# Spike counts and membrane reset of a spiking recurrence: bfloat16 count on VectorE, spike taken from v - 1 written by ScalarE

## The chip, the core and the metric

The kernel runs on one core of a Trainium2 chip. The metric is the device time in microseconds, median of several executions. The engines that appear below are PE (TensorE, matrix products and transposes), VectorE (DVE), ScalarE (ACT), GpSimd (POOL, here the issuer of the gathers) and SyncE (SP, issuer of the stores). They run their own instruction streams and wait for one another through semaphores. SBUF is the on-chip memory, PSUM the eight banks that PE writes its results to.

## The reference

Of the reference only one sequence model matters: 1024 sequences of 50 item numbers, a table of 100001 embeddings of 128 numbers, scores for all items.

```python
emb = emb_table.at[0].set(0.0)
e = emb[seq]                                   # (1024, 50, 128)
prefix = jnp.cumsum(e, axis=1)
denom = jnp.minimum(t_idx[None, :], lengths[:, None])
uF = prefix / denom[:, :, None]
mean = uF.mean(axis=0)
var = uF.var(axis=0)
y = (uF - mean) * lax.rsqrt(var + BN_EPS) * gamma + beta
def step(v, x):
    v = v + (x - v) / TAU                      # TAU = 2
    spike = atan_spike(v - V_TH)               # 1 where v >= 1
    v = v - lax.stop_gradient(spike) * V_TH
    return (v, spike)
_, spikes = lax.scan(step, v0, x_seq)          # 50 steps
uF_out = spikes.mean(axis=0)                   # (1024, 128)
scores = uF_out @ emb.T                        # (1024, 100001)
```

So for each of 50 steps the running mean of the gathered embeddings is normalised over the batch, fed into a leaky integrator with a threshold, and the spikes are counted. The counts, divided by 50, are multiplied with the whole table.

## The kernel before

The kernel has two stages. In the first, the recurrence, everything lies transposed: 128 embedding dimensions on the partitions, 1024 sequences along the row, in two halves of 512 that fit a PSUM bank each. In the second the counts are the stationary operand and the table, split into a high and a low part, is multiplied with them block by block, scaled by 1/50 on VectorE and ScalarE in turn (L469, L471), and stored by SP (L161).

The order of the instructions on each engine is that of the program; nothing reorders them. For the recurrence it is written by hand. Step t of the loop (L288) does this:

- POOL issues the eight gathers of step t + 2 (L194), 128 table rows each, into one of three buffers e. It may begin when the transposes of step t - 1 have read that buffer.
- PE transposes the eight blocks of e(t) and adds them to the running sum in PSUM, `pre[0]` and `pre[1]` (L301). A correction by PE (`correct`, L257) takes out row 0 of the table in advance; its factor l is made by ScalarE (`only`, L252).
- VectorE multiplies each half with the reciprocal length (L310, giving uF) and takes batch statistics of it (L311), then the mean and the variance mv (L321).
- ScalarE takes the square root (L325) and subtracts the mean from uF (L326). Meanwhile VectorE computes s, the spikes of the previous step, as bfloat16 zeros and ones from v in PSUM (L331), and PE adds them up by a product with the identity matrix (`counted`, L268) into two PSUM banks `sums` over all steps.
- VectorE finishes the scale a of the normalisation (L334 to L340).
- ScalarE writes x, the scaled uF, into the PSUM tile v of this step (`x`, L344; v lies in two tiles in turn, v0 and v1). Meanwhile VectorE computes negv = s - v of the previous step (L353).
- VectorE finishes the step, v = x - negv/2 (`step`, L347).

The sign of negv makes the reset and the leak one operation. In the last step, t = 49, s and negv of step 48 are computed at the top of the loop's body (L295, L296), and the sums of steps 0 to 48 are copied from PSUM by ScalarE into a tile `count` (L319). The spikes of step 49 are added to it in three groups of columns (`spiked`, L279), which gives the operands of the products. Before these, PE runs sixteen transposes of the identity matrix (`warm`, L378) while it waits.

In steps 42 and 44 the first two blocks of the table are also transposed and split (`prepare`, L122, L144, L145), with tile v1 as their place in PSUM.

The two lines on which the counting rests before:

```python
nc.vector.tensor_single_scalar(s, v, V_TH, ALU.is_ge)
nc.vector.tensor_tensor(negv, s, v, ALU.subtract)
```

Of the kernel before, what the change touches and what calls it, by code (L numbers as in the profile page):

```python
# [12 lines left out]
F32 = mybir.dt.float32  # L13
BF16 = mybir.dt.bfloat16
# [3 lines left out]
AF = mybir.ActivationFunctionType  # L18
ALU = mybir.AluOpType

P = 128
BN_EPS = 1e-5
V_TH = 1.0
HALF = 1024
KQ = HALF // P
BANK = 512
# [9 lines left out]
def rec_kernel(  # L36
# [9 lines left out]
    nc = tc.nc  # L46
    B, T = seq.shape
# [20 lines left out]
    ident = const.tile([P, P], F32, tag="ident", name="ident")  # L68
# [80 lines left out]
    def product(po, q, n, k0, kw):  # L149
        kw += kw % 2  # L150
        for j, part in enumerate(split[q]):
            nc.tensor.matmul(  # L152
                po[:, :kw],
                lhsT=counts[n],
                rhs=part[:, k0 : k0 + kw],
                start=j == 0,
                stop=j == 1,
            )
# [4 lines left out]

    with ExitStack() as ph:
        once = ph.enter_context(tc.tile_pool(name="once", bufs=1))
        lp = ph.enter_context(tc.tile_pool(name="lif", bufs=2))
        sp = ph.enter_context(tc.tile_pool(name="stats", bufs=3))
        up = ph.enter_context(tc.tile_pool(name="uF", bufs=2))
        gp = ph.enter_context(tc.tile_pool(name="gather", bufs=3))
        accp = ph.enter_context(tc.tile_pool(name="acc", bufs=1, space=bass.MemoryType.PSUM))  # L170
# [20 lines left out]
        def gather(t):  # L191
            es[t] = gp.tile([P, B], F32, tag="e", name=f"e_{t}")
            for n in range(NB):
                nc.gpsimd.indirect_dma_start(  # L194
                    out=es[t][:, n * P : (n + 1) * P],
                    out_offset=None,
                    in_=table,
                    in_offset=bass.IndirectOffsetOnAxis(ap=idx[:, n, t : t + 1].bitcast(U32), axis=0),
                )
# [12 lines left out]
        zT = once.tile([P, B], F32R, tag="zT", name="zT")  # L212
# [23 lines left out]
        nc.vector.tensor_scalar_mul(hgb[:, 1:2], gb[:, 1:2], 0.5)  # L236
        eps = once.tile([P, 1], F32, tag="eps", name="eps")
        nc.vector.memset(eps, BN_EPS)
        ident_h = once.tile([P, P], BF16, tag="ident_h", name="ident_h")
        nc.vector.tensor_copy(ident_h, ident)  # L240

        negv = once.tile([P, B], F32, tag="negv", name="negv")
        nc.vector.memset(negv, 0.0)


        pre = [accp.tile([P, BANK], F32, tag=f"pre{h}", name=f"pre{h}") for h in range(B // BANK)]
        sums = [accp.tile([P, BANK], F32, tag=f"sums{h}", name=f"sums{h}") for h in range(B // BANK)]

        def only(t):

# [12 lines left out]
                    skip_group_check=True,  # L263
                )

        def counted(t, s):
            for h in range(B // BANK):
                nc.tensor.matmul(  # L268
                    sums[h],
                    lhsT=ident_h,  # L270
                    rhs=s[:, h * BANK : (h + 1) * BANK],
                    start=t == 0,
                    stop=t == T - 2,
                    skip_group_check=True,
                )


        def spiked(out, cs, v):
            nc.vector.scalar_tensor_tensor(out, v, V_TH, count[:, cs], ALU.is_ge, ALU.add)  # L279

        whole = slice(0, B)
        halves = [slice(h * BANK, (h + 1) * BANK) for h in range(B // BANK)]
        v = None
# [4 lines left out]
        for t in range(T):  # L288
            last = t == T - 1
            if t + 2 < T:  # L290
                gather(t + 2)
            e = es.pop(t)
            if last:
                s = lp.tile([P, B], BF16, tag="s", name=f"s_{t - 1}")
                nc.vector.tensor_single_scalar(s, v, V_TH, ALU.is_ge)  # L295
                nc.vector.tensor_tensor(negv, s, v, ALU.subtract)  # L296
            uF = up.tile([P, B], F32, tag="uF", name=f"uF_{t}")
            bs = sp.tile([P, B // BANK, 6], F32, tag="bs", name=f"bs_{t}")
            for h, cs in enumerate(halves):
                for k in range(0, BANK, P):  # L300
                    nc.tensor.matmul(  # L301
                        pre[h][:, k : k + P],
                        lhsT=e[:, h * BANK + k : h * BANK + k + P],
                        rhs=ident,
                        start=False,
                        stop=last,
                        is_transpose=True,
                        skip_group_check=True,
                    )
                nc.vector.scalar_tensor_tensor(uF[:, cs], rlen[:, cs], 1.0 / (t + 1), pre[h], ALU.max, ALU.mult)  # L310
                nc.vector.bn_stats(bs[:, h, :], uF[:, cs])  # L311
            if not last:
                correct(t + 1, l)
            else:

                counted(t - 1, s)
                count = once.tile([P, B], F32, tag="zT", name="count")
                for h, cs in enumerate(halves):
                    nc.scalar.copy(count[:, cs], sums[h])  # L319
            mv = sp.tile([P, 2], F32, tag="mv", name=f"mv_{t}")  # L320
            nc.vector.bn_aggr(mv, bs.rearrange("p h s -> p (h s)"))  # L321


            r = sp.tile([P, 1], F32, tag="r", name=f"r_{t}")
            nc.scalar.activation(r, mv[:, 1:2], AF.Sqrt, bias=eps)  # L325
            nc.scalar.activation(uF, uF, AF.Identity, bias=mv[:, 0:1], scale=-1.0)  # L326


            if t and not last:
                s = lp.tile([P, B], BF16, tag="s", name=f"s_{t - 1}")  # L330
                nc.vector.tensor_single_scalar(s, v, V_TH, ALU.is_ge)  # L331
                counted(t - 1, s)

            nc.vector.reciprocal(r, r)  # L334
            q = sp.tile([P, 1], F32, tag="q", name=f"q_{t}")
            nc.vector.tensor_mul(q, r, r)  # L336
            nc.vector.scalar_tensor_tensor(q, mv[:, 1:2], BN_EPS, q, ALU.add, ALU.mult)  # L337
            nc.vector.tensor_scalar(q, q, -0.5, 1.5, ALU.mult, ALU.add)
            a = sp.tile([P, 1], F32, tag="a", name=f"a_{t}")
            nc.vector.tensor_scalar(a, q, r, hgb[:, 0:1], ALU.mult, ALU.mult)  # L340


            def x(vt, cs):
                nc.scalar.activation(vt, uF[:, cs], AF.Identity, bias=hgb[:, 1:2], scale=a)  # L344

            def step(vt, cs):
                nc.vector.scalar_tensor_tensor(vt, negv[:, cs], -0.5, vt, ALU.mult, ALU.add)  # L347

            if not last:
                vt = vp.tile([P, B], F32, tag=f"v{t % 2}", name=f"v_{t}")  # L350
                x(vt, whole)
                if t:
                    nc.vector.tensor_tensor(negv, s, v, ALU.subtract)  # L353
                step(vt, whole)
                v = vt
                if t + 2 < T:
                    l = only(t + 2)

                if t in (T - 8, T - 6):
                    q = (t - T + 8) // 2  # L360
                    pair(q)
                    prepare(q, vp.tile([P, HALF], F32, tag="v1", name=f"pt_{q}"))
                    if q == TWICE - 1:
                        for k in range(TWICE):
                            rows[GROUP + k] = first[:, k, :]
                        nc.sync.dma_start(
                            out=first[:, :TWICE, :],
                            in_=table[GROUP * HALF : (GROUP + TWICE) * HALF, :].rearrange(
                                "(q p k) d -> p q (k d)", p=P, k=KQ
                            ),  # L370
                        )
# [15 lines left out]
        cs, vt, first = groups[0]  # L387
# [5 lines left out]
            spiked(c, cs, vt)  # L393


        po1 = vp.tile([P, HALF], F32, tag="v0", name="po_0_1")
        for q, (pool, tag, po) in enumerate(((gp, "e", sums), (up, "uF", [po1[:, cs] for cs in halves]))):
            o = pool.tile([P, HALF], F32, tag=tag, name=f"o_0_{q}")
            for h, cs in enumerate(halves):
                product(po[h], q, 0, h * BANK, BANK)  # L400
            for h, cs in enumerate(halves):
                if q and h:
                    nc.vector.tensor_scalar_mul(o[:, cs], po[h], 1.0 / T)
                else:
                    nc.scalar.mul(o[:, cs], po[h], 1.0 / T)
                store(0, q * HALF + h * BANK, o[:, cs])


# [16 lines left out]
    for c, W in enumerate(WIDTHS):  # L425
# [30 lines left out]
        for n in range(NB):  # L456
            if c == 0 and n == 0:
                continue
            pool, tag, most = turns[blocks % len(turns)]
            blocks += 1  # L460
            o = pool.tile([P, most * HALF], F32, tag=tag, name=f"o_{c}_{n}")
            for q in range(q0, q1):
                h0 = (q - q0) * HALF
                hw = size(q)
                po = psum.tile([P, HALF], F32, tag="ps", name=f"po_{n}_{q}")
# [45 lines left out]
```

## Time and profile before

| | us |
|---|---|
| median of three runs | 1652.33 (1652.13 to 1652.79) |
| the profiled execution | 1650.34 |
| its span, first to last instruction | 1648.6 |
| VectorE busy | 940.2 (57%) |
| PE busy | 1101.3 (67%) |
| ScalarE busy | 631.1 (38%) |
| POOL busy | 378.4 (23%) |
| gathers, L194, 400 of them | 377.7, mean 0.944 |
| spikes s, L331, 48 of them in the loop | 56.2, mean 1.170 |
| negv, L353, 48 | 58.1, mean 1.211 |
| step, L347, 47 | 57.8, mean 1.229 |
| counting on PE, L268, 128x512 each | mean 0.606 |

How to read the views: the page cuts the span into 40 slices, each digit the busy share of an engine in a slice in tenths. A timeline line gives start, length, engine, line of the program, operation, tiles written and read, and in brackets how long the engine had been idle before and what released it. "issue" means that the profile shows nothing that it waited for, "remote" that the releasing instruction wasn't found. In the chain of waits the same case is called "another core or an unknown queue"; here there is one core only. A table of stages gives, after the length of the stretch, busy time and number of instructions of PE, its weight loads, VectorE, ScalarE and POOL, then the granted clock of PE, the busy share of the DMA engines and GB/s. The records of matrix products are partly modelled: their starts and ends can lie before the real ones.

### The profile page before, as it was taken

The page shows a single profiled execution, that of the slowest core. Times are in us where ns is not written, and L with a number is a line of the kernel's source. Part 1 is how long each engine was busy: PE and PEld are TensorE (multiplying, and loading weights), DVE is VectorE, ACT ScalarE, POOL GpSimd, SP SyncE. Part 2 cuts the span into 40 slices and gives each one's busy share as a digit, 9 for nine tenths or more (in the row PEclk, how much of TensorE's full clock was granted, in tenths as well). Part 3 has the DMA queues.
Part 4 walks back from the last instruction along what each step waited for, and adds up shares of the span by engine and source line. Part 5 has one row for each costly group of instructions (what it writes and reads, how often), then busy time and mean ns, then how long its engine had stood idle before and what let it go on. Part 6 is the DMA issues. An engine that isn't in the chain of part 4 may idle for free.

```text
span 1648.6 us, 12553 instructions
## 1 busy us (share of the span) xinstructions
PE 1101.3 (67%) x4538; PEld 825.5 (50%) x4548; DVE 940.2 (57%) x1161; ACT 631.1 (38%) x700; POOL 378.4 (23%) x406
## 2 busy tenths in 40 slices
PE   3333443333333488888987887888787887888884
PEld 2112222122222366666876666666666666666763
DVE  4556666566656766556755555555555555555552
ACT  2222222222222355445544444444444444444442
POOL 7666666666666500000000000000000000000000
PEclk6555555555555589999999999989989999999998
DMA  9511111111111269999999999999999999999998
GB/s 341 214 48 43 48 47 48 48 43 48 48 47 45 64 275 417 403 423 416 399 429 427 431 432 424 422 422 418 421 427 423 430 417 410 427 427 423 396 429 343
DMA packets 53691, 488.14 MB, mean 296 GB/s; under 512 B 11995, under 2 KB 12796, under 8 KB 32380
## 3 DMA queue, kind: packets, MB, share of 16 engines
q1 hardware_dynamic: 32256, 429.81, 62.1%
q0 software_dynamic: 12800, 26.24, 5.9%
q10 hardware_dynamic: 8572, 31.28, 4.7%
q8 instruction: 36, 0.59, 0.1%
q14 instruction: 27, 0.22, 0.0%
HBM read 77.69 MB, written 409.60 MB: 296 GB/s over the span
## 4 chain that ended last, share of the span: by engine, by line
DMA 47%; DVE 22%; another core or an unknown queue 10%; PE 10%; ACT 6%; issue 4%; POOL 0%; ACTq 0%; DVEq 0%; SPq 0%
DMA scores<-o 46%; PE po L152 9%; ACT o L471 5%; DVE bs L311 4%; DVE uF L310 4%; DVE v L347 4%; DVE s L331 3%; DVE negv L353 3%; DVE o L469 1%; DVE a L340 1%; DVE mv L321 1%; ACT v L344 1%; DVE q L337 0%; DVE q L336 0%
## 5 line engine op out<-in xcount | busy, mean ns | idle before, releaser
L469 DVE TENSOR_SCALAR o<-po 128x1024 f32<-128x1024 f32 x391 | 464.1, 1221 | 351.3 <-DMA scores<-o 311.3
L471 ACT ACTIVATE o<-po 128x1024 f32<-128x1024 f32 (+1 forms) x391 | 389.1, 1018 | 542.9 <-DMA scores<-o 325.5
L194 POOL DMA_INDIRECT e<-in_L_rec_emb_table,idx x400 | 377.7, 944 | 188.2 <-issue 114.9
L152 PE MATMUL po<-pairs,countB 128*128 128x512 f32 x1136 | 306.3, 416 | 63.2 <-ACT o L471 46.5
L152 PEld LDWEIGHTS po<-pairs,countB 128*128 128x128 f32 x1136 | 219.3, 198 | 126.3 <-ACT o L471 61.2
L152 PE MATMUL po<-pairs,countC 128*128 128x512 f32 x852 | 229.7, 415 | 55.0 <-ACT o L471 54.9
L257 PE MATMUL pre<-zT,l 128*128 128x512 f32 x100 | 74.7, 749 | 275.6 <-DVE uF L310 188.6
L152 PEld LDWEIGHTS po<-pairs,countC 128*128 128x128 f32 x852 | 162.3, 197 | 99.5 <-ACT o L471 66.6
L257 PEld LDWEIGHTS pre<-zT,l 128*128 128x128 f32 x100 | 27.7, 279 | 316.9 <-issue 210.7
L310 DVE SCALAR_TENSOR_TENSOR uF<-rlen,pre 128x512 f32<-128x512 f32 x100 | 68.0, 680 | 185.3 <-remote 144.1
L325 ACT ACTIVATE r<-mv,eps 128x1 f32<-128x1 f32 x50 | 14.7, 295 | 383.5 <-DVE mv L321 266.3
L145 DVE TENSOR_TENSOR pairs<-pt,pairs 128x1024 fp32r<-128x1024 f32 x71 | 86.3, 1222 | 89.6 <-ACT pairs L144 89.5
L122 PE MATMUL pt<-ident,rows 128*128 128x128 f32 x782 | 109.4, 286 | 5.0 <-issue 3.2
L122 PEld LDWEIGHTS pt<-ident,rows 128*128 128x128 f32 x782 | 99.2, 150 | 23.3 <-issue 8.4
L301 PE MATMUL pre<-ident,e 128*128 128x128 f32 x400 | 98.4, 419 | 10.8 <-DMA e<-in_L_rec_emb_table,idx 6.8
L301 PEld LDWEIGHTS pre<-ident,e 128*128 128x128 f32 x400 | 86.1, 226 | 34.9 <-issue 25.7
L152 PE MATMUL po<-hi,countB 128*128 128x512 f32 x216 | 89.8, 416 | 17.2 <-ACT o L471 14.4
L268 PE MATMUL sums<-s,ident_h 128*128 128x512 bf16 x88 | 45.3, 606 | 64.2 <-issue 33.1
L152 PE MATMUL po<-lo,countB 128*128 128x512 f32 x216 | 86.6, 403 | 0.0
L152 PE MATMUL po<-hi,countC 128*128 128x512 f32 (+1 forms) x162 | 68.0, 420 | 13.7 <-ACT o L471 13.7
L144 ACT CAST pairs<-pt 128x1024 fp32r<-128x1024 f32 x71 | 71.8, 1011 | 13.9 <-PE pt L122 13.7
L152 PE MATMUL po<-pairs,countA 128*128 128x512 f32 x284 | 71.7, 395 | 8.1 <-ACT o L471 8.1
(76 smaller groups left out, 872.8 us busy)
## 6 DMA issues: line engine op xcount, KB each, us to landing
scores<-o SPq DMA_DIRECT2D x96, 3072.0 KB, 19.8
scores<-o SPq DMA_DIRECT2D x32, 1536.0 KB, 9.0
scores<-o SPq DMA_DIRECT2D x30, 1024.0 KB, 8.6
rows<-in_L_rec_emb_table ACTq DMA_DIRECT2D x19, 1536.0 KB, 29.1
scores<-o SPq DMA_DIRECT2D x8, 2896.5 KB, 17.4
rows<-in_L_rec_emb_table SPq DMA_DIRECT2D x6, 3072.0 KB, 33.9
e<-in_L_rec_emb_table,idx POOLq DMA_INDIRECT x400
rows<-in_L_rec_emb_table SPq DMA_DIRECT2D x1, 1024.0 KB
```

Source lines behind the costliest of these rows:

```text
L122: nc.tensor.transpose(pt[:, k0 : k0 + kw], r[:kw, k0 : k0 + D], ident[:kw, :kw])
L144: nc.scalar.copy(vh, vp)
L145: nc.vector.tensor_tensor(vl, vp, vh.bitcast(F32), ALU.subtract)
L152: nc.tensor.matmul(po[:, :kw], lhsT=counts[n], rhs=part[:, k0 : k0 + kw], start=j == 0, stop=j == 1,)
L194: nc.gpsimd.indirect_dma_start(out=es[t][:, n * P : (n + 1) * P], out_offset=None, in_=table, in_offset=bass.IndirectOffsetOnAxis(ap=idx[: ...
L257: nc.tensor.matmul(pre[h], lhsT=l, rhs=zT[:, h * BANK : (h + 1) * BANK], start=t == 0, stop=False, skip_group_check=True,)
L301: nc.tensor.matmul(pre[h][:, k : k + P], lhsT=e[:, h * BANK + k : h * BANK + k + P], rhs=ident, start=False, stop=last, is_transpose=True, ...
L310: nc.vector.scalar_tensor_tensor(uF[:, cs], rlen[:, cs], 1.0 / (t + 1), pre[h], ALU.max, ALU.mult)
L311: nc.vector.bn_stats(bs[:, h, :], uF[:, cs])
L347: nc.vector.scalar_tensor_tensor(vt, negv[:, cs], -0.5, vt, ALU.mult, ALU.add)
L469: nc.vector.tensor_scalar_mul(o[:, h0 : h0 + hw], po[:, :hw], 1.0 / T)
L471: nc.scalar.mul(o[:, h0 : h0 + hw], po[:, :hw], 1.0 / T)
```

## The change

The count moves from PE to VectorE: `count` is a bfloat16 tile that starts at zero, and `spiked` adds the comparison of v with the threshold to it, once a step, in the place where negv was computed. The numbers are whole and at most 50, which bfloat16 holds exactly. The comparison inside negv is no longer the tile s. Right after a step ScalarE writes d = v - 1 as bfloat16 (`over`), and one step later negv = (d >= 0) - v is computed in one operation (`rest`), in the place where s was computed. The tile pool of d has one buffer, where that of s had two. The PSUM tiles `sums`, the identity matrix in bfloat16, `counted` and the copies from `sums` are gone; the first output block of the products gets a PSUM tile `po0` of two banks in place of the two tiles `sums`.

```diff
-        lp = ph.enter_context(tc.tile_pool(name="lif", bufs=2))
+        lp = ph.enter_context(tc.tile_pool(name="lif", bufs=1))
...
-        ident_h = once.tile([P, P], BF16, tag="ident_h", name="ident_h")
-        nc.vector.tensor_copy(ident_h, ident)
+        less = once.tile([P, 1], F32, tag="less", name="less")
+        nc.vector.memset(less, -V_TH)
+        count = once.tile([P, B], BF16, tag="count", name="count")
+        nc.vector.memset(count, 0.0)
...
-        sums = [accp.tile([P, BANK], F32, tag=f"sums{h}", name=f"sums{h}") for h in range(B // BANK)]
...
-        def counted(t, s):
-            for h in range(B // BANK):
-                nc.tensor.matmul(
-                    sums[h],
-                    lhsT=ident_h,
-                    rhs=s[:, h * BANK : (h + 1) * BANK],
...
+        def over(t, v):
+
+            d = lp.tile([P, B], BF16, tag="d", name=f"d_{t}")
+            nc.scalar.activation(d, v, AF.Identity, bias=less)
+            return d
+
+        def rest(d, v):
+            nc.vector.scalar_tensor_tensor(negv, d, 0.0, v, ALU.is_ge, ALU.subtract)
...
             if last:
-                s = lp.tile([P, B], BF16, tag="s", name=f"s_{t - 1}")
-                nc.vector.tensor_single_scalar(s, v, V_TH, ALU.is_ge)
-                nc.vector.tensor_tensor(negv, s, v, ALU.subtract)
+                rest(d, v)
+                spiked(count, whole, v)
...
-            else:
-
-                counted(t - 1, s)
-                count = once.tile([P, B], F32, tag="zT", name="count")
-                for h, cs in enumerate(halves):
-                    nc.scalar.copy(count[:, cs], sums[h])
...
             if t and not last:
-                s = lp.tile([P, B], BF16, tag="s", name=f"s_{t - 1}")
-                nc.vector.tensor_single_scalar(s, v, V_TH, ALU.is_ge)
-                counted(t - 1, s)
+                rest(d, v)
...
                 if t:
-                    nc.vector.tensor_tensor(negv, s, v, ALU.subtract)
+                    spiked(count, whole, v)
                 step(vt, whole)
                 v = vt
+                d = over(t, v)
                 if t + 2 < T:
                     l = only(t + 2)
...
+        po0 = accp.tile([P, HALF], F32, tag="po0", name="po_0_0")
         po1 = vp.tile([P, HALF], F32, tag="v0", name="po_0_1")
-        for q, (pool, tag, po) in enumerate(((gp, "e", sums), (up, "uF", [po1[:, cs] for cs in halves]))):
+        for q, (pool, tag, po) in enumerate(((gp, "e", po0), (up, "uF", po1))):
```

More of the change, by code (lines that the diff above doesn't have):

```diff
@@ L264, in correct @@
                 )
-        def counted(t, s):
-            for h in range(B // BANK):
-                nc.tensor.matmul(
-                    sums[h],
-                    lhsT=ident_h,
-                    rhs=s[:, h * BANK : (h + 1) * BANK],
[L272 to L275, printed above, removed]
+        def over(t, v):
[4 more added lines that the diff above has]
+            nc.vector.scalar_tensor_tensor(negv, d, 0.0, v, ALU.is_ge, ALU.subtract)
         def spiked(out, cs, v):
@@ L393, in rec_kernel @@
             spiked(c, cs, vt)
+        po0 = accp.tile([P, HALF], F32, tag="po0", name="po_0_0")
         po1 = vp.tile([P, HALF], F32, tag="v0", name="po_0_1")
-        for q, (pool, tag, po) in enumerate(((gp, "e", sums), (up, "uF", [po1[:, cs] for cs in halves]))):
+        for q, (pool, tag, po) in enumerate(((gp, "e", po0), (up, "uF", po1))):
             o = pool.tile([P, HALF], F32, tag=tag, name=f"o_0_{q}")
             for h, cs in enumerate(halves):
-                product(po[h], q, 0, h * BANK, BANK)
+                product(po[:, cs], q, 0, h * BANK, BANK)
             for h, cs in enumerate(halves):
                 if q and h:
-                    nc.vector.tensor_scalar_mul(o[:, cs], po[h], 1.0 / T)
+                    nc.vector.tensor_scalar_mul(o[:, cs], po[:, cs], 1.0 / T)
                 else:
-                    nc.scalar.mul(o[:, cs], po[h], 1.0 / T)
+                    nc.scalar.mul(o[:, cs], po[:, cs], 1.0 / T)
                 store(0, q * HALF + h * BANK, o[:, cs])
```

## Prediction

> **What bounds the kernel now.** I read the page first, then the clock of the one core, the stages, the chain of waits inside the recurrence, the timeline around one of its stalls, and last the gathers alone. The page shows two halves. From 0 to about 585 us POOL is busy and the DMA engines are nearly idle; afterwards POOL is silent and the DMA engines are full.
>
> ```profile
> PE   3333443333333488888987887888787887888884
> POOL 7666666666666500000000000000000000000000
> DMA  9511111111111269999999999999999999999998
> ```
>
> The second half is bound by the stores (the chain's largest entry is 46% "DMA scores<-o"), and the change doesn't touch it, so what matters is when it starts. The first half is the 50 steps of the recurrence. The chain of waits there, over one step and the stall that follows it (start, length, what):
>
> ```profile
> 314.75 1.09 DVE s L331
> 316.79 1.14 DVE negv L353
> 318.13 1.23 DVE v L347
> 319.35 7.03 another core or an unknown queue
> 326.41 0.69 DVE uF L310
> 327.13 0.69 DVE bs L311
> 327.83 4.22 another core or an unknown queue
> 332.05 0.69 DVE uF L310
> ```
>
> Two of three steps run back to back on VectorE, 7.49 us each (the second halves' L310 at 305.62 and 313.10). In the third VectorE stands still for 7.03 + 4.22 = 11.25 us. The timeline of the same place says what it stands for:
>
> ```profile
> 316.69 1.91 PE L301 MATMUL pre<-ident,e 128*128 128x128 f32 x8
> 318.32 0.94 POOL L194 DMA_INDIRECT e<-in_L_rec_emb_table,idx  x1 [0.30 <-issue]
> 326.41 0.69 DVE L310 SCALAR_TENSOR_TENSOR uF<-rlen,pre 128x512 f32<-128x512 f32 x1 [7.06 <-remote]
> 327.07 0.94 POOL L194 DMA_INDIRECT e<-in_L_rec_emb_table,idx  x1 [0.30 <-issue]
> 332.04 0.69 DVE L310 SCALAR_TENSOR_TENSOR uF<-rlen,pre 128x512 f32<-128x512 f32 x1 [4.21 <-remote]
> 332.28 0.94 POOL L194 DMA_INDIRECT e<-in_L_rec_emb_table,idx  x1 [4.27 <-remote]
> ```
>
> VectorE and POOL wait for the same event and go on within 0.24 us of each other: the transposes of this step (L301), which feed L310 and, once done, free the gather buffer that POOL wants. The matmul records put the eight transposes at 316.69, but their release comes piecemeal until 332.0, that is until 4.0 us after POOL's issues stopped (327.07 + 0.94 = 328.0). I can't name the cause of that hold. But its sum is regular. The stages cut at POOL's restarts:
>
> ```profile
> 298.35:332.28 33.93, 12.84 (x36) 7.70 (x36) 21.30 (x40) 8.60 (x12) 22.65 (x25) 0.50 0.18 47
> 468.06:502.05 33.99, 12.24 (x36) 7.42 (x36) 21.30 (x40) 8.60 (x12) 22.67 (x25) 0.55 0.18 47
> 502.05:524.75 22.70, 9.47 (x31) 6.41 (x32) 15.65 (x29) 6.74 (x9) 15.10 (x16) 0.58 0.17 46
> ```
>
> A stretch with three steps has 24 gathers and takes 33.93 us, 1.414 us a gather; one with two steps has 16 and takes 22.70, 1.419; the first, from 4.2 to 60.8 us with 40 gathers and hardly three steps of compute, 1.413. So the time goes with the number of gathers and not with what PE, ACT or VectorE did between: 400 x 1.414 = 566 us from 4.2 is 570, where VectorE's last stall ends (570.02). POOL issues one every 1.25 us, and the stall (3.0 us after 16, 4.3 after 24, 6.7 after 40) brings it to 1.41. VectorE needs 3 x 7.49 = 22.5 of each 33.93 us: the slack is 11.4 us in three steps, 3.8 in one.
>
> **What the Trainium skill says.** "VectorE: DVE Perf Modes", section on the perf-mode tier table with "Why PSUM operands drop a tier": an fp32 operand in PSUM holds VectorE to one element a cycle, whatever the other operand is. The trace agrees: L353 reads bf16 s beside v in PSUM and takes 1211 ns, L331 writes bf16 and takes 1170, L347 is all fp32 and takes 1229. "ScalarE: Activation LUTs", section "What ACT_TABLE_LOAD costs": about 280 ns + 0.833 ns an element with a bias read from a tile, 1133 ns for 1024; L326, of that form, takes 1.13 us. "SBUF — State Buffer", section "SBUF: two separate sides": VectorE locks GpSimd out in two-port modes or with two SBUF inputs. The new instructions read one operand from PSUM, so no lock is expected; L194 is 938 to 953 ns whatever VectorE does.
>
> **The change, part by part.** All in the profiled execution: 1650.34 us, of which 1648.6 is the span. The median of the runs is 1652.33, 1.99 above it; the shift is added to that.
>
> *Inside a step, VectorE.* In the slot of s (L331, 1170 ns, beside ScalarE's square root and mean subtraction) now stands negv from d and v, a scalar_tensor_tensor with one PSUM operand. In the slot of negv (L353, 1211 ns, beside ScalarE's x) stands the count. No row has these operands exactly; the nearest run from 1170 to 1229 ns and I take 1220 for both. That is +0.05 us in the first slot. The second ends by 302.97 where x ends at 303.12 (L344, 301.91 + 1.21), so the step still starts with x. A step becomes 7.54 us; over 48 steps 2.4 us if nothing hid it, and it lies in the 3.8 us of slack.
>
> *Inside a step, ScalarE.* One new activation d behind step, 1.13 us (from L144's 1.01 to L344's 1.21), and behind it on the same queue l (L252, 0.39), which used to run during step. ScalarE's next work, r, waits for mv, 2.9 us after step's end (304.38 to 307.26); d and l take 1.6. l is needed by the correction (L257): it comes at 306.0 instead of 305.1, about 1 us late, and the transposes behind it on PE are wanted only at 311.78. Free, as is the single buffer of d: its reader is done over 3 us before the next write.
>
> *Inside a step, PE.* Two counting matmuls (1.01 us for the pair) go. They held the queue: the transposes of the next step stood behind them until s was done, 316.69; now they follow the correction directly, at about 314.4, 2.3 us earlier. In the two quick steps nobody waits for them, and in the third, by the stretches above, the end is set by the gathers. Worth nothing in the sum; the bounds are in the rivals.
>
> *Before the loop.* One bf16 memset of 1024 in place of a 128-wide cast: at most the 0.91 us of negv's memset, before L310 at 14.78, whose second half waits anyway (3.01 us at 19.20).
>
> *The last step*, with no slack left, because no gathers remain. Before: step 48 ends at 577.60, s 577.64, negv 578.90, L310 at 580.12 on the chain. Now negv must wait for d: 577.60 + 0.09 to ScalarE (the gap from a to x) + 1.13 + 0.03 back = 578.85; negv 1.22 to 580.07, the count 1.22 to 581.29. So +1.2 us (1.0 with d at L144's price, 1.3 at L344's), and 0.05 from step 48. What goes there (two matmuls, two ScalarE copies of 0.59) lay beside VectorE and gives nothing. The warm-up transposes and the first product move by the same. From 602 us on stores follow each other on the chain, so a later start is a later end.
>
> *The ends of po.* One tile of two banks instead of two of one: if its halves were waited for together, 0.8 us (586.50 to 587.28) on a first store that isn't on the chain: 0.
>
> Sum: +1.2, so 1651.5 for the profiled execution and 1652.33 + 1.2 = 1653.5 for the median.
>
> **Rivals.**
> Stalls shrink (faster): the hold could have a length of its own, counted from where the transposes start, and would then end up to 2.3 us sooner in each of some 14 stretches: -32 + 1.2, 1621.5. For it: VectorE and POOL wait for just these transposes. Against: step 43's began at 517.57, were free at 524.5, after 6.9 us, while step 26's took 15.3; both end 3 to 4 us after POOL's last issue. 15%, partial gains included.
> Shorter stretches (slower): the hold strikes the second step too, POOL runs out of buffers after 16 gathers, and the 1.419 to 1.425 of those (22.70 and 22.80) replaces 1.414 to 1.416 over 376 gathers: up to 3.4 us more, with the last step's 1.2 1657. It decides from transposes that start more than some 13 us into a stretch (step 45's were held at 13.9); the second step's start at 10.9 now and 8.6 then, so it should get rarer. 14%, with a first product that finds the slower clock after the moved warm-up, some 1.7 us.
> PE was the bound: 48 x 1.01 = 48 us, 1605. PE is busy 12.84 of 33.93 us: 1%.
> The forecast, all hidden but the last step: 70%.
>
> **How the numbers follow.** About 0.2%, 3.3 us, is what a measurement can tell from no change. The likeliest case is +1.2 with 1.0 to 1.4 from d and some 2 us either way from the clock and the cutting of stretches: 1651 to 1656. To leave out no more than 2 in 10 the range takes in the slower rival and the smaller gains of the faster one: 1647 to 1658. Faster 16%, within 0.2% 67%, slower 17%: the last takes the second rival and a little of the first case's upper end.
>
> **What would show it.** Right: L194's restarts still 33.9 us apart with 24 gathers, VectorE's idle before L310 about 11 us in three steps, the last L310 1.2 us later behind a wait for d, the same distance from there to the end. Wrong: stalls under 3 us after 24 gathers (the faster rival), restarts 22.7 apart throughout (the slower), an L194 over 0.95 us (a lock after all), or a count far from 1.22 us.

## The result and the profile after

| | before | after |
|---|---|---|
| median of 20 runs each, us | 1652.28 | 1651.0 |
| lowest to highest | 1650.7 to 1659.22 | 1648.81 to 1654.14 |
| profiled execution | 1650.34 | 1651.18 |
| its span | 1648.6 | 1649.4 |

The ratio is 0.9985, 95% interval 0.9976 to 0.9994: some 2.5 us faster, between 1.0 and 4.0. The medians differ by 1.3 us. Four of the 20 runs of before stand in a group near 1658 us and none of the changed kernel's; this group, whose cause no trace shows, makes about half of the ratio's 2.5 (without these four runs the means differ by 1.2 us). The forecast was 1.2 us slower, so the sign is wrong. 1651.0 lies within its range, 1647 to 1658, but that range is wide enough to hold both signs.

The two profiled executions differ the other way, by 0.84 us, so the profile has to be read by its stages. The shape of the page is the same: gathers first, stores after. From the list of groups, the gathers and the new work of ScalarE (busy, mean ns of one, then idle time before them):

```profile
L194 POOL DMA_INDIRECT e<-in_L_rec_emb_table,idx x400 | 378.6, 946 | 187.0 <-issue 114.0
...
L270 ACT ACTIVATE d<-v,less 128x1024 bf16<-128x1024 f32 x49 | 54.6, 1114 | 65.9 <-DVE v L336 39.9
```

A gather costs POOL what it cost before (944 ns before, 946 after), so VectorE's new instructions do not lengthen it. On VectorE negv takes 1.17 us in the loop and the count 1.22. Then the stages of the changed kernel, cut again at POOL's restarts:

```profile
298.45:343.65 45.20, 12.46 (x40) 8.83 (x40) 28.46 (x53) 15.78 (x20) 30.28 (x33) 0.54 0.18 46
...
524.53:547.13 22.60, 8.38 (x29) 6.29 (x29) 17.53 (x30) 9.29 (x12) 15.13 (x16) 0.50 0.32 94
```

Here is what the prediction did not foresee. A stretch no longer holds three steps and 24 gathers in 33.93 us, but four steps and 32 gathers in 45.1 to 45.5 (ten stretches of this kind). Per gather that is 1.410 to 1.421 against 1.414: hardly anything, since POOL's stall grew nearly in proportion, from 4.2 or 4.3 us to between 5.4 and 5.7. The timeline of one stretch, which began at 253.31, says how it came about:

```profile
269.37 1.91 PE L298 MATMUL pre<-ident,e 128*128 128x128 f32 x8
...
274.22 0.68 DVE L307 SCALAR_TENSOR_TENSOR uF<-rlen,pre 128x512 f32<-128x512 f32 x1
...
277.12 1.91 PE L298 MATMUL pre<-ident,e 128*128 128x128 f32 x8
...
291.89 0.69 DVE L307 SCALAR_TENSOR_TENSOR uF<-rlen,pre 128x512 f32<-128x512 f32 x1 [9.37 <-issue]
...
298.22 0.69 DVE L307 SCALAR_TENSOR_TENSOR uF<-rlen,pre 128x512 f32<-128x512 f32 x1 [4.92 <-remote]
298.45 0.95 POOL L194 DMA_INDIRECT e<-in_L_rec_emb_table,idx  x1 [5.42 <-remote]
```

The third step's transposes stand 16.1 us into the stretch (269.37 - 253.31) and get through: VectorE takes their first half at 274.22 without a wait, and over the ten stretches the second half comes between 0 and 3.2 us late. The fourth step's, 23.8 us in, are held until 298.2. In the kernel before, the third step's stood 18.3 us in (316.69 - 298.35) and were held for 15.3. The two differ by the 2.3 us for which the counting products had held PE's queue; experiment 5 tests whether that is the cause.

The end of the recurrence in the chain of waits of the changed kernel:

```profile
567.42 1.23 DVE v L336
568.65 0.60 DVE uF L307
...
574.93 1.24 DVE v L336
576.20 1.12 ACT d L270
577.34 1.22 DVE negv L274
578.56 1.14 DVE count L277
...
582.37 0.22 DVE mv L312
...
585.27 3.79 PE po L152 x8
...
602.83 7.43 DMA scores<-o
```

Step 48 starts its uF directly behind the step before it (567.42 + 1.23 = 568.65). In the kernel before VectorE stood still there for 1.47 us:

```profile
567.33 1.23 DVE v L347
568.56 1.47 another core or an unknown queue
570.03 0.69 DVE uF L310
```

In the last step VectorE waits for d from 576.17 (574.93 + 1.24) to 577.34, 1.17 us, where before s followed within 0.04.

### The profile page after: what moved, and what is told of

Read it like the earlier page. It is cut to its first block, busy times and chain, and to the rows that moved or that the text cites. A ratio compares the mean times of both kernels' runs of the same rounds, so it can differ in the third digit from the quotient of the medians.

```text
span 1649.4 us, 12367 instructions
## 1 busy us (share of the span) xinstructions
PE 1052.7 (64%) x4450; PEld 812.8 (49%) x4450; DVE 941.0 (57%) x1162; ACT 683.0 (41%) x747; POOL 379.3 (23%) x406
## 4 chain that ended last, share of the span: by engine, by line
DMA 44%; DVE 21%; another core or an unknown queue 11%; PE 11%; ACT 7%; issue 3%; POOL 0%; ACTq 0%; SPq 0%; DVEq 0%
DMA scores<-o 44%; PE po L152 11%; ACT o L462 5%; DVE bs L308 4%; DVE uF L307 4%; DVE v L336 4%; DVE negv L274 3%; DVE count L277 2%; ACT v L333 1%; DVE o L460 1%; DVE a L329 1%; DVE mv L312 1%; DVE q L326 0%; DVE q L325 0%
## 5 line engine op out<-in xcount | busy, mean ns | idle before, releaser
L258 PE MATMUL pre<-zT,l 128*128 128x512 f32 x100 | 69.7, 755 | 379.6 <-DVE uF L307 208.8
L152 PE MATMUL po<-pairs,countC 128*128 128x512 f32 x852 | 234.7, 422 | 50.5 <-ACT o L462 50.5
L152 PEld LDWEIGHTS po<-pairs,countC 128*128 128x128 f32 x852 | 165.8, 201 | 96.2 <-ACT o L462 62.0
L270 ACT ACTIVATE d<-v,less 128x1024 bf16<-128x1024 f32 x49 | 54.6, 1114 | 65.9 <-DVE v L336 39.9
```

Of the source, the lines that this page charges most:

```text
L152: nc.tensor.matmul(po[:, :kw], lhsT=counts[n], rhs=part[:, k0 : k0 + kw], start=j == 0, stop=j == 1,)
L258: nc.tensor.matmul(pre[h], lhsT=l, rhs=zT[:, h * BANK : (h + 1) * BANK], start=t == 0, stop=False, skip_group_check=True,)
```

## The experiments

All ran beside the kernel before on the same chip. "Restart" is the moment at which POOL takes up the gathers for the last time, "last mv" the mv of step 49, which ends the recurrence.

**1. The place of the products alone.** In the kernel before, the counting products are issued one step later, behind the next step's transposes.

```diff
+            if pending:
+                counted(*pending)
+                pending = None
             if not last:
                 correct(t + 1, l)
...
-                counted(t - 1, s)
+                pending = t - 1, s
```

> The kernel before with one move: PE's two counting products of a step are issued one step later, behind the next step's transposes, so that these no longer stand in the queue behind s. PE does the same work, VectorE and ScalarE too. Theory A (the place in PE's queue is what the change gains by): POOL's stretches become 32 gathers long as in the kernel after, the stall of 1.46 us before L310 in step 48 goes, and the time is 1.4 us under the kernel before, about 1650.9. Theory B (the gain is the PE work itself, two products a step less): stretches of 24 as before, the stall stays, 1652.3. Theory C (the gain is noise of the second half): stretches change or not, no difference in time beyond 0.5 us.

Measured: 1652.59 us of 22 runs, ratio 1.0008 (0.9998 to 1.0019). A miss. The stretches became irregular, 8, 16, 24 and 32 gathers, so the place does decide where the hold strikes; but no time was won, and the restart came at 549.13, later than before. From there to the last mv it took 34.40 us, less than the 35.24 to 35.56 of the five traces of the kernel before, so at the end the earlier transposes did win. Six of the 22 runs lie near 1660, as a group of the kernel before does near 1658. The chain of waits in its step 48 shows the price of the new place:

```profile
570.87 1.15 PE pre L257
572.02 0.68 DVE uF L311
```

The products now stand ahead of the correction (L257), and VectorE waits for PE between the halves. So the run is no clean test; experiment 5 is.

**2. The wait for d filled.** In the changed kernel, the last step counts first and takes negv afterwards.

```diff
-                rest(d, v)
                 spiked(count, whole, v)
+                rest(d, v)
```

> The kernel after with one swap: at the top of the last step the count of step 48 comes before negv, so that VectorE counts while ScalarE still writes d. Theory A (the wait for d in the last step is on the path, 1.14 us in the trace of after): the last batch aggregate comes 1.1 us earlier than in after (582.4 to 581.3) and the time is 1.1 us under after, about 1649.9. Rival (something else ends last there, the transposes or the stores): same as after, 1651.0.

Measured: 1651.41 of 22, ratio 0.9988 (0.9981 to 0.9996): no gain. The chain:

```profile
578.22 1.12 ACT d L270
579.36 1.23 DVE count L277
580.59 1.13 DVE negv L274
```

The count starts only behind d as well, though it doesn't read it; the trace doesn't show why. Swapping moved the wait from one instruction to the other; VectorE stands still for the same 1.1 us.

**3. The gathers taken away.** Half of the gathers in both kernels; the transposes of the second half of the columns read the first half again.

```diff
-            for n in range(NB):
+            for n in range(NB // 2):
...
-                        lhsT=e[:, h * BANK + k : h * BANK + k + P],
+                        lhsT=e[:, k : k + P],
```

> The kernel before with half of its gathers: only the first four blocks of a step's rows are gathered, and each is transposed twice, so the computed numbers are those of half the batch repeated. 200 gathers need 283 us at 1.414 us each, below 50 steps of VectorE's 7.49 us. Theory A (the gathers set the first half's time): no long stalls, a step every 7.49 us, the first half ends some 175 us earlier and the time is near 1475. Rival (VectorE, ScalarE and PE set it, the stalls being theirs): the stalls stay and the time is within 20 us of 1652.

> The kernel after with half of its gathers, as in e3_before_half, so with the same half of the batch repeated. With the cover of the gathers gone the step's own price shows. Theory A (the two new VectorE operations cost what the two old ones did, a step stays 7.49 us): 1.1 us over e3_before_half, the wait for d in the last step alone. Rival as predicted (each step 0.05 us longer, hidden in the full kernel): 3.5 us over it. Rival (the step is shorter without the counting products): under it.

Measured: 1466.24 (before, ratio 0.8869, 0.8853 to 0.8886) and 1468.5 (after, 0.8881, 0.8865 to 0.8897), four runs each. With 200 gathers fewer the recurrence ends 181 to 184 us earlier. So gathers, not compute, set the first half in both kernels. Nearly every step now takes 7.48 to 7.49 us in both: the new VectorE instructions cost what the old ones did. The medians differ by 2.3 us, more than the 1.1 that the first theory said, and the last mv of the two traces by 2.47 (398.59 and 401.06). The largest part lies on the chain of the last step. The kernel before with half the gathers:

```profile
392.17 1.24 DVE v L347
...
395.91 0.61 DVE uF L310
```

and the changed kernel with half of them:

```profile
393.62 1.24 DVE v L336
394.88 1.12 ACT d L270
396.03 1.22 DVE negv L274
397.25 1.14 DVE count L277
398.39 0.60 DVE uF L307
```

From the start of v to uF it is 3.74 us against 4.77, so the wait for d costs 1.0 us. A further 0.64 comes in step 44, where d stands ahead of ScalarE's copy for the preparation of the table (10.45 to 11.09 us), a place that is hidden when gathers are whole; and 0.8 in the first steps.

**4. The output block in two tiles.** The changed kernel with the first output block in two PSUM tiles of one bank, as before.

```diff
-        po0 = accp.tile([P, HALF], F32, tag="po0", name="po_0_0")
...
+                product(po[h], q, 0, h * BANK, BANK)
```

> The kernel after with the first output block in two PSUM tiles of a bank each, as before, in place of po0. Theory A (the single tile makes ScalarE wait for all four products of the block: the first store is 5.6 us behind the last batch aggregate in after, 4.3 in before): 4.3 again, the second half 1.3 us shorter, the time about 1649.8. Rival (the prediction's: the first store isn't on the path): no difference to after, 1651.0.

Measured: 1650.22 of 14, ratio 0.9987 (0.9977 to 0.9997). The first store starts 4.79 us behind the last mv and not 5.64, but from the last mv to the end it is 1066.88 against 1067.04. The two-bank tile costs nothing, as forecast.

**5. The wait put back.** To experiment 4's kernel two products per step are added on PE at the old place, which wait for VectorE's negv as the counting waited for s. Nobody uses them.

```diff
                 rest(d, v)
+                for h in range(B // BANK):
+                    nc.tensor.matmul(
+                        sums[h],
+                        lhsT=ident_h,
+                        rhs=negv.bitcast(BF16).rearrange("p (n two) -> p n two", two=2)[:, h * BANK : (h + 1) * BANK, 1],
...
```

> e5_twopo, and PE does two products of the size of the counting ones again at their old place, behind negv in VectorE's order (of the upper halves of negv's words; their result isn't used). They hold the next step's transposes back as the counting did. All else is e5_twopo. Theory A (what the change gains in the first half is that the transposes no longer wait there): stretches of 24 gathers, the stall of 1.5 us before L310 in step 48 back, and some 2 to 4 us over e5_twopo, with single runs 6 us up as before has them. Rival (the place in PE's queue is worth nothing, as predicted): same as e5_twopo within 0.5 us.

Measured: 1652.21 of 14, ratio 0.9998 (0.9989 to 1.0007), 2.0 us over experiment 4, measured beside it. A stage between two of its restarts:

```profile
298.46:332.42 33.96, 11.94 (x36) 7.40 (x36) 21.30 (x40) 11.84 (x15) 22.72 (x25) 0.55 0.18 47
```

This is the stretch of the kernel before, 24 gathers in 34 us; 13 of its stretches are of that kind. And the chain at its end has the stall of step 48 again:

```profile
567.55 1.23 DVE v L349
568.78 1.56 another core or an unknown queue
570.34 0.69 DVE uF L311
...
584.12 0.22 DVE mv L316
```

VectorE and ScalarE do the changed kernel's work here; only PE has its old place in the order back. The whole gain is gone: the median is 0.5 us above that of the kernel before (1651.69 of 43). The run puts back the wait and 1 us of PE work a step together, and doesn't tell these two apart; experiment 1 speaks for the place, since it left PE's work as it was and still changed the stretches. The group near 1658 did not come back in these 14 runs, where the kernel before beside them has it in 9 of 43; so what makes the group isn't shown to be the place in the queue.

**6. The last step without d.** Experiment 4's kernel, with s and negv of step 48 computed by VectorE as before, and s added to the count later, behind a, beside ScalarE.

```diff
             if last:
-                rest(d, v)
-                spiked(count, whole, v)
+                s = lp.tile([P, B], BF16, tag="d", name="s_last")
+                nc.vector.tensor_single_scalar(s, v, V_TH, ALU.is_ge)
+                nc.vector.tensor_tensor(negv, s, v, ALU.subtract)
...
+            if last:
+                nc.vector.tensor_tensor(count, count, s, ALU.add)
```

> e5_twopo, and in the last step VectorE takes the spikes of step 48 itself: s and negv as before, and s is added to the count from SBUF while ScalarE works on x. There is no d of step 48 to wait for. Theory A (the wait for d costs the last step 11.03 instead of 10.01 us): 1.0 us less than e5_twopo, 1648.8 if that is 1649.8. Rival (the stores decide the end): no difference.

> e6_own once more, beside the two others on the same chip: 1649.5, ratio to the kernel before 0.998, first eight products 3.8 us, 20.5 us from the last mv to the first large store. Theory and rival say the same here.

Measured: 1649.48 of 22, ratio 0.9980 (0.9972 to 0.9988), and in a repetition 1650.21 of 22, 0.9985 (0.9978 to 0.9993). Its chain:

```profile
574.75 1.24 DVE v L341
576.02 1.24 DVE s_last L295
577.28 1.22 DVE negv L296
578.50 0.61 DVE uF L310
...
582.79 0.60 DVE count L334
```

Uninterrupted VectorE; the last step takes 10.0 us again, not 11.0. The addition of 0.60 us stands on the chain at 582.79, where I had counted it as hidden: hence 0.74 won over experiment 4, not 1.0. This is the fastest version of all, though its lead over the changed kernel is below what these runs separate.

**7. Does the hold need the gathers' data?** The changed kernel with transposes that read the reciprocal lengths; the gathers run on and nobody reads them.

```diff
-                        lhsT=e[:, h * BANK + k : h * BANK + k + P],
+                        lhsT=rlen[:, h * BANK + k : h * BANK + k + P],
```

> The kernel after, but the transposes of the recurrence read the tile of reciprocal lengths and not the gathered rows, which nobody reads; the scores are of other numbers. POOL waits for PE no longer, and PE doesn't wait for gathers. Theory A (the hold strikes PE's releases whatever PE reads, as long as gathers keep coming): VectorE still stalls before L307 in some steps, some 14 us and more into POOL's work, until POOL's last gather near 504 us. Theory B (the hold belongs to the gathered data): no stalls, a step every 7.49 us, the last batch aggregate near 400 us while POOL still issues.

Measured: 1863.58, one run. The windows of its trace:

```profile
100.00:128.00 28.00, 3.27 (x10) 2.21 (x10) 7.24 (x14) 3.94 (x5) 20.99 (x24) 1.00 0.20 52
...
600.00:628.00 28.00, 11.88 (x40) 8.83 (x40) 26.42 (x51) 14.57 (x19) 0.00 (x0) 0.56 0.00 0
```

While gathers flow, a step takes 28.0 us, and VectorE waits for the transposes for 241 us between 100 and 500 us (24 waits of up to 11.3), though no transpose reads a gathered row. The gathers ran with hardly a stop, the first 160 at 1.25 us each (4.15 to 204.12) and later at 1.40 in a steady pattern (20 in 28.00 us), the last ending at 538.1. So 1.25 us can be kept up for 200 us when POOL doesn't have to wait for buffers. After the last gather one more step of 28 us followed; from 566 the steps take 7.5 us again. So the hold is no wait for the rows: here PE's results come late while gathers run, though PE reads nothing that they write. What holds them, and why it outlasts the last gather by one step here, stays open.

**8. The kernel before once more**, four times without an edit, to see how its restarts and its end scatter.

> The kernel before again, unchanged, for another trace: its first one ran 1650.34 us, 2 us under the median of its runs. Theory A (the first half varies from run to run with the place at which POOL's stretches are cut): a run near 1652.3 shows other stretches and a later last restart of POOL than 547.55, by as much as it is slower. Rival (the second half varies): the same stretches, and a second half longer than 1065.8 us from the last batch aggregate to the end.

> The kernel before, unchanged, for another trace. About one run in six of it lies near 1658 instead of 1651.7, which no run of after or of e7_hold did. If this is such a run: theory A says that the stretches are cut otherwise at the end, so that three steps instead of two are left when the last hold ends (7.5 us); the rival says that the second half is longer. If not: stretches of 24 and a last restart within 1 us of 547.6.

> As b_look1: the kernel before, unchanged, for another trace, with the same expectations.

> As b_look1: the kernel before, unchanged, for another trace, with the same expectations.

Measured: 1650.24, 1650.8, 1652.12 and 1651.16, one run each; none fell in the group near 1658. The slowest has the same stretches as the first profile and a second half that is longer (1066.69 us from the last mv to the end, against 1065.78), as the rival said. Together with the first profile, and beside the changed kernel and its kin, all in us:

| traces | restart | last mv | last mv to the first large store on the chain | from there to the end |
|---|---|---|---|---|
| before, mean of 5 | 548.10 | 583.46 | 19.53 (18.82 to 20.28) | 1046.2 |
| after | 547.13 | 582.37 | 20.46 | 1046.6 |
| count first (2) | 549.18 | 584.40 | 20.76 | 1046.2 |
| two tiles (4) | 546.97 | 582.16 | 20.49 | 1046.4 |
| wait put back (5) | 547.78 | 584.12 | 19.68 | 1046.1 |
| last step without d (6) | 546.97 | 581.18 | 20.47 | 1046.3 |

In its own trace the changed kernel reaches its last mv 1.1 us sooner than the mean of before, but experiment 2's, the same program up to the last step, restarts 2.0 us later (549.18 against 547.13) and has no such lead: one trace is too few for the first half. Between the last mv and the stores the changed kernel loses 0.9. The cause of this loss is in the first products. One execution of before has, in its chain:

```profile
586.40 1.15 PE sums L152 x4
587.55 0.92 PE po L152 x4
...
602.25 8.55 DMA scores<-o
```

Eight products in 2.07 us at the full clock, where the changed kernel's chain has 3.79 at half. Of the five traces of before, two have the full clock there (distance 18.8), two a mixture (19.8 and 19.9), one 3.59 us (20.28); of the changed kernel and its kin with whole gathers, only experiment 5's is a mixture (2.86 us); the others take 3.5 to 3.8.

**9. PE kept busy ahead of the products.** 24 more transposes of the identity in the last step, behind those of e, in experiment 6's kernel and in experiment 4's.

```diff
             if not last:
                 correct(t + 1, l)
+            else:
+                for k in range(24):
+                    nc.tensor.transpose(sums[k // 4 % 2][:, k % 4 * P : (k % 4 + 1) * P], ident, ident)
```

> e6_own with 24 more transposes of the identity on PE in the last step, right behind the transposes of e(49) and ahead of the warm-up; nobody reads their result before the products overwrite the place. Theory: the second half of the changed kernel is 1.0 to 1.2 us longer because PE does nothing for some 5 us before the warm-up, so that its clock is still at half when the first products run (eight of them 3.8 us in place of 2.1). Then the clock is granted in full before the products, the first eight take 2.1 us, from the last mv to the first large store on the chain it is 18.8 us in place of 20.5, and the time is 1.0 to 1.7 us under e6: about 1648.2. Rival: the excess lies elsewhere in the second half, or the granted clock doesn't follow this work: the first eight products still 3.8 us or the distance still 20.5, the time that of e6.

> e5_twopo (the changed kernel with the first output block in two one-bank tiles) with the same 24 transposes. Theory: as there, first eight products 2.1 us, 18.8 us from the last mv to the first large store, 1.0 to 1.7 us under e5: about 1649. Rival: time of e5, 1650.2.

Measured: 1649.84 of 22, ratio 0.9986 (0.9979 to 0.9994), and 1650.85 of 22, 0.9987 (0.9979 to 0.9996). No gain over experiment 6, repeated beside them (0.9985), nor over experiment 4 (0.9987). The first eight products still run at half clock, and the distance is 20.8 and 20.7 us. The windows of the first of the two (PE's busy time is the first number behind the comma, its clock the third from the end):

```profile
569.65:573.06 3.41, 3.28 (x12) 2.59 (x13) 3.21 (x8) 1.34 (x2) 0.00 (x0) 0.50 0.00 0
573.06:576.47 3.41, 2.61 (x24) 2.37 (x22) 3.13 (x5) 1.21 (x1) 0.00 (x0) 1.00 0.00 0
576.47:579.89 3.42, 1.38 (x13) 1.38 (x14) 3.35 (x5) 0.00 (x0) 0.00 (x0) 1.00 0.00 0
579.89:583.30 3.41, 1.03 (x6) 0.63 (x4) 2.84 (x9) 1.76 (x4) 0.00 (x0) 0.50 0.00 0
583.30:586.71 3.41, 2.67 (x6) 2.15 (x7) 2.86 (x7) 2.48 (x5) 0.00 (x0) 0.50 0.02 5
```

The clock was at full from 573 to 580, too early: at the first product (584.04) it was back at half. My theory, that PE's idleness before the warm-up decides, has fallen in this form: the added transposes filled the window 569.65 to 573.06, and of the two just ahead of the products one held 1.38 us of PE's work and the other 1.03. That the half clock of the first products goes with the longer distance holds in every trace.

The traces also show what the clock follows; the rule is worked out from them alone. In all 17 of them it changes only on a grid of 3.41 us, whose position against the program differs from execution to execution, and in each window of the grid it goes with PE's busy share in the window before. At half clock, a window with PE busy for 90% or more was followed by full clock every time (529 of 529), one with less than 65% never (0 of 1860); in between both occur. At full clock it stayed up behind every window with 55% or more and behind none with less than 40%. Cut on this grid, first an execution of the kernel before (the first of experiment 8), then the changed kernel:

```profile
581.09:584.50 3.41, 3.19 (x16) 2.78 (x14) 2.88 (x8) 0.83 (x2) 0.00 (x0) 0.50 0.00 0
584.50:587.91 3.41, 1.51 (x7) 1.30 (x8) 2.63 (x8) 3.04 (x6) 0.00 (x0) 1.00 0.00 0
...
578.69:582.10 3.41, 2.35 (x11) 2.35 (x12) 3.34 (x5) 0.00 (x0) 0.00 (x0) 0.50 0.00 0
582.10:585.51 3.41, 1.56 (x8) 1.16 (x7) 2.15 (x10) 2.74 (x5) 0.00 (x0) 0.50 0.00 0
585.51:588.93 3.42, 3.42 (x9) 2.64 (x10) 2.00 (x4) 1.44 (x3) 0.00 (x0) 0.50 0.01 5
```

In the first, the warm-up fills 3.19 of 3.41 us and the products (from 586.40) find the full clock. In the second the warm-up is split over two windows, 2.35 us in the one, and they find half. In experiment 5 the same warm-up, with no counting in the last step either, lay in one window (3.24 us), and the products began at full. So the 0.9 us depend, at least in part, on where the grid lies. Whether the change makes the bad case more frequent, by taking the last counting products (1 us) from in front of the warm-up, these few traces don't show.

## Why the prediction was wrong

The failed step is this one: "Inside a step, PE ... In the two quick steps nobody waits for them, and in the third, by the stretches above, the end is set by the gathers. Worth nothing in the sum". It put the earlier start of the transposes at nothing; experiment 5, which puts the wait and the two products back together, measures it at 2.0 us (medians 1652.21 and 1650.22), more than the 1.2 us of cost that the prediction set against it. In the third step the 2.3 us decide. Its transposes move from 18.3 to 16.1 us into the stretch and come through at most 3.2 us late, where before they were held for 15.1 to 15.6. The prediction's rival asked what the earlier start does to the second step (10.9 to 8.6 us) and not what it does to the third; by its own mark, "some 13 us", the third would have been held at 16.1 as well. No single mark fits the traces: in a stretch of 16 gathers transposes were held at 14.0.

Where the 2.0 us lie can be told in part. Inside the recurrence the consequence is small, because the time per gather stays at 1.41 us: the last restart comes at 547.49 on average in the seven traces of the changed kernel and its kin with PE's queue free (546.97 to 549.18), at 548.10 in the five of before (547.55 to 548.58), which the scatter doesn't separate. At the end the consequence is clear, because step 48 is no longer held: from the last restart to the last mv it is 35.19 to 35.25 us in four traces of the changed kernel (its own, experiments 2 and 4, the second kernel of experiment 9) and 36.34 with the wait put back, 1.1 us. The wait for d takes nearly as much back: without it (experiment 6, twice, and the first kernel of experiment 9) it is 34.12 to 34.21. Hence before (35.24 to 35.56) and after hardly differ there.

The other steps of the prediction:

- VectorE's new instructions, "it lies in the 3.8 us of slack": right. Steps without gathers in the way take 7.49 us (forecast 7.54), and before as after. The Trainium skill, "VectorE: DVE Perf Modes", perf-mode tier table, was the ground for pricing the new instructions like the old, and 1.17 and 1.22 us bear it out for a bf16 operand beside an fp32 one in PSUM.
- ScalarE's d and l, "free": right inside the loop. The mean of d is 1114 ns, forecast 1.13 us.
- "The last step", +1.2: right in kind, 1.0 us by experiments 3 and 6.
- "The ends of po ... 0": right (experiment 4).
- "the same distance from there to the end": wrong in the traces by 0.9 us. The prediction had named a first product at the slower clock, "some 1.7 us", only as an accident in the slower rival. 3.79 - 2.07 = 1.72 us is what it costs where the execution compared has the full clock. By the traces under experiment 9 it depends on where the clock's grid lies.
- The rival "Stalls shrink": wrong. A stall after 32 gathers is longer than one after 24. The rival "Shorter stretches" had the mechanism, a hold that strikes by when transposes start, and the wrong direction, though it noted that "it should get rarer".

One account doesn't close. In the traces the 1.1 us won and the 0.9 lost nearly cancel, and the five traced executions of before lie at 1650.2 to 1652.1, all under its median of 1652.28; the untraced runs are 1.3 us faster after, and the run with the wait put back 2.0 us slower than its twin, close to the difference of their last mv alone (584.12 - 582.16 = 1.96). The grid of the clock offers an answer: the second half takes 1065.0 to 1065.2 us from the last mv where the first products find the full clock, 1065.8 to 1065.9 in a mixture and 1066.6 to 1067.0 at half, in the kernel before (1065.0 to 1066.7) as in the others. If the untraced runs meet these cases about equally often before and after, the 0.9 us drop out. Which clock they had, no run here shows.

## What to carry to other kernels

When a queue is freed earlier, ask of every step in a repeating pattern, not only of those that run freely, whether the new start falls on the other side of a recurring stall; then look at the last repetition, where nothing evens it out. A pace that goes with the number of gathers hides what is won inside it, but not what is won after the last of them. Before a difference of a microsecond between two traces is put down to a change, look at the granted clock of the first products in several executions of each kernel.

## What the hardware showed that was not expected

- With gathers running without a pause, PE's results reached VectorE so late that a step took 28.0 us in place of 7.5, though PE read no gathered data (experiment 7). With stretches of 24 or 32 gathers, the second half of uF came 3.9 to 4.2 us (before) or 6.2 (after) behind transposes that began up to 11 us into a stretch, 6.2 to 9.4 behind those at 16.1 us, and 15.1 to 15.6 behind those at 18.3. The cause was not found.
- The time per gather, 1.41 us, is the same with 16, 24 and 32 between stalls, while POOL issues one in 1.25. With half of the gathers POOL's stall was 2.8 us after every four. It is not the most that gathers can do: in experiment 7 the first 160 went at 1.25 us each without a stall.
- The granted clock of PE was full while PE was nearly idle and at half while it worked without a gap: it is fixed for windows of 3.41 us and goes with PE's busy share in the window before. In experiment 9 the window 576.47 to 579.89 ran at full, behind one with 2.61 us of work, and PE was busy for 1.38; in the changed kernel 585.51 to 588.93 ran at half, behind one with 1.56, and PE was busy throughout.
